# A first group cut into four tasks, other step orders at the layer change and in layer 1, and no restoring identity products: two chained GNN layers on one core

## The chip, the cores and the metric

The kernel runs on one core of a Trainium2 chip. The metric is the device time of one execution in microseconds (us), as the median of several executions. Lower is better.

## The reference

`x` is 128 graphs of 128 nodes with 512 features, `adj` 128 dense 128x128 adjacency matrices, all fp32. Layer 0 is a mean aggregation, layer 1 an attention-weighted diffusion with three hops. Both are followed by a residual and a layernorm:

```python
# layer 0
agg = einsum('bij,bjf->bif', adj, x) / max(sum(adj, -1), 1e-6)
x   = layernorm(x + relu(concat([x, agg], 2) @ W.T))          # W: 512 x 1024
# layer 1
Xw  = x @ Wv + bv                                             # used only through aw
e   = leaky_relu(sj[:, None, :] + si[:, :, None] + ab, 0.2)   # sj = Xw @ aw[:d], si = Xw @ aw[d:]
T   = adj * exp(e);  T = T / (sum(T, -1) + 1e-12)
H = 0; Xk = x
for k in range(3):
    H = H + Xk @ Wk[k] + bk[k]
    Xk = T @ Xk
x   = layernorm(x + relu(H))
```

## The kernel before

**Groups.** The 128 graphs are worked in 32 groups of 4 (`NG`, `G`): 32 periods of layer 0, then 32 of layer 1. The result of layer 0 goes through DRAM (`yd`) and is read back for layer 1, whose group 0 therefore needs only the early groups of layer 0.

**Products.** The large products with the weights are done by a scheme of seven products in place of eight block products, on two levels. The outer level gives tasks (`P12`, `P56`, `P74` and `T` in layer 0; `O1` to `O7` in layer 1), the inner level gives each task seven steps. A step is the matmuls of one inner product (`prod`, all recorded at line L149) and then the small work that this product releases. In layer 1 every `O` task runs `outer` (L605 to L641): after step 1 ScalarE copies bank X to Y (L617), after step 2 it copies Z to `s5` (L623), after step 3 VectorE adds W = X + s5 (L626), after step 5 it makes the sum Z directly (L650 or L663). Step 3 accumulates into X and must wait until the copy of step 1 has read it. Step 5 accumulates into X and must wait for the add of step 3, and step 7 for the direct sum of step 5. Steps 4 and 6 need the banks filled by the copy of step 1 and the add of step 3. `O5` starts its bank X from a copy of the folded bias (`beta`, L615). The tasks of kind `adding` also have GpSimd add into `s5` after step 3 (L660), and step 5's sum needs that. `C` combines the three hops (eight steps `c.1` to `c.8`, products with the transition matrix).

**Banks and lanes.** PSUM holds eight banks, four named bA and four named bB. Each four are a lane. A lane carries one task at a time, and two lanes alternate so that one task's small work lies beside the other's matmuls. All banks are first written by an identity product (L146).

**The order is written by hand.** `PA` (32 steps) is the order of a layer-0 period, `PT` that of the turn from layer 0 to layer 1, `PB` (57 steps) that of a layer-1 period, `PL` that of the last. In them a name with a small letter (`p74.6`, `t.1`, `o3.7`, `c.5`) is a step of the group before. In layer 1 the first group runs `PB` from `O5.1` on. Everything else (loads, transposes L254, left-side sums L242 to L277, layernorm L488 to L506, attention scores L712 to L721) is put beside the steps by `at` and `place`: the tables `START`, `PLACES_A`, `PLACES_B`, `PLACES_T`, `PLACES_M` and `PLACES_L` give each operation a position in half-steps. The engines run in the order so emitted: there is no scheduler that moves instructions.

```python
for t, (lane, name, g, k) in enumerate(steps):
    ...
    next(gens[name, g], None)                        # the step's matmuls and small work
    run([(f, *args) for f, args in beside.pop(2 * t, ())])
    run(late)                                        # evictions that wait for this step
    run([(f, *args) for f, args in beside.pop(2 * t + 1, ())])
```

**The start.** Group 0 of layer 0 has no aggregation task beside it. A task `F` (function `first`, 14 steps in bA) makes two columns of seven products, each product for the upper half `xu` and the lower half `xl` of the group's graphs. Its first step needs both. The group's first two transposes give `xu`, the next two `xl`; GpSimd makes the inner sums (`x_inner`, L242 to L245), VectorE the inner differences of the weights (`w_inner`, L931 to L934) and two of the outer ones (`w_outer`, L939). Bank set bB takes `fold_constants` meanwhile: biases and attention vectors are folded in seven small pieces (`fold`), and at the end two identity products (L184) write the two banks that the folding had used. `FL` then multiplies by the adjacency.

Of the kernel before, what the change touches and what calls it, by code (L numbers as in the profile page):

```python
# [8 lines left out]
FP = mybir.dt.float32  # L9
# [7 lines left out]
def kernel(  # L17
# [14 lines left out]
    nc = tc.nc  # L32
    P = 128
# [8 lines left out]
    R = 32  # L42
# [67 lines left out]
    wvt_sb = [p2.tile([P, 2, F], FP, name=f"wvt{i}", tag="y") for i in range(2)]  # L110
# [3 lines left out]
    bk_sb = p1.tile([K, F], FP, name="bk_sb", tag="TT")  # L114
# [5 lines left out]
    load_w0([nc.scalar], 1)  # L120
    load_w0([nc.scalar], 3)
    load_adj(0)
    for i in range(2):
        nc.sync.dma_start(wvt_sb[i], wvt[i * FH : (i + 1) * FH, :].rearrange("(c p) f -> p c f", p=P))
# [32 lines left out]
    def fold_constants():  # L157
        ones_row = ones[:].to_broadcast([P, P])
        pb, pc, pw = bB[0], bB[3], bB[0]
# [17 lines left out]
        w2row = p1.tile([2, NC, Q, R], FP, name="w2row", tag="TT")  # L177
# [5 lines left out]
        for t in (pw, pc):  # L183
            nc.tensor.matmul(t, ident, ident[:, None, :].to_broadcast([P, Q, P]), start=True, stop=True)  # L184
# [72 lines left out]
    def x_inner(n, p):  # L257
        need(("x_turn", n, p, 1))
        t = (xu, xl)[p][n]
        left_sums([S_, S_, S_, S_], [t[:, :, i] for i in range(7)])  # L260
# [71 lines left out]
    def p12(lane, g):  # L332
        r, c11 = rs[g], c11s[g] = blocks(p2, "r"), blocks(p2, "c11")

        def evict(b, t):
            L_.copy(part(r, b), t[:, :FH])
            V.tensor_add(part(c11, b), t[:, FH:], part(r, b))
        yield from pair(lane, g, 1, 2, evict)
# [10 lines left out]
    def p74(lane, g):  # L349
        r, c22, c21 = rs[g], blocks(p2, "c22"), blocks(p2, "c21")  # L350
        c22s[g], c21s[g] = c22, c21

        def evict(b, t):
            need(("P56", g, {BY: 4, BWW: 6, BZ: 7, BX: 7}[b]))
            L_.copy(part(c22, b), t[:, :FH])
            V.tensor_add(part(c21, b), t[:, FH:], part(r, b))
            V.tensor_add(part(c21, b), t[:, :FH], part(c21, b))
        yield from pair(lane, g, 7, 4, evict)
# [68 lines left out]
    def first(lane, g):  # L427
        c11, c21 = blocks(p2, "c11"), blocks(p2, "c21")
        c11s[g], c21s[g] = c11, c21

        def column(o, bank_of, evict):
            X, Y, W, Z = [bA[i] for i in bank_of]

            def prod(dst, k, start=False):
                for h in range(2):
                    for i in range(2):
                        mm(dst[:, h * FH : (h + 1) * FH], (xu, xl)[h][g][:, i, LEFT[k]], wf[:, SLOT[2 * i + o], RIGHT[k]],
                           start and i == h == 0)
            s5 = halves()
            prod(X, 1, True)  # L440
            L_.copy(Y, X)
            yield
            prod(Z, 5, True)
            L_.copy(s5, Z)
            yield
            prod(X, 6)
            V.tensor_add(W, X, s5)
            yield
            prod(Y, 2)
            yield  # L450
            prod(X, 7)
            evict(BY, Y)
            V.tensor_add(Z, X, s5)
            yield
            prod(W, 3)
            yield
            prod(X, 4)
            evict(BWW, W)
            evict(BZ, Z)
            late.append((evict, BX, X))  # L460
            yield

        def evict0(b, t):
            L_.copy(part(c11, b), t[:, :FH])
            V.tensor_copy(part(c21, b), t[:, FH:])
        yield from column(0, (0, 1, 2, 3), evict0)

        def evict1(b, t):
            i, h = b
            L_.copy(bB[i][:, h * FH : (h + 1) * FH], t[:, :FH])  # L470
            V.tensor_copy(bB[2 + i][:, h * FH : (h + 1) * FH], t[:, FH:])
        yield from column(1, (1, 2, 0, 3), evict1)
        lane[:] = [bA[2], bA[3], bA[1], bA[0]]

    def first_last(lane, g):
        new_mv(g)
        for p, t in ((1, c21s[g]), (0, c11s[g])):
            for i in range(2):
                b = 2 * p + i
                mm(bB[b], aTs[g][:, b], t[:, i, :, :FH])  # L480
                late.append((residual, g, b, bB[b]))
            yield
        lane[:] = [bB[2], bB[0], bB[1], bB[3]]
# [326 lines left out]
    TASKS = {"F": first, "FL": first_last, "P12": p12, "P56": p56, "P74": p74, "T": last, "O1": o1, "O2": o2, "O5": o5,  # L810
             "O6": o6, "O7": o7, "O4": o4, "O3": o3, "C": combine}
    lanes = [list(bA), list(bB)]
    steps = []

    def step(lane, name, g, k):
        steps.append((lane, name, g, k))

    PA = "p74.5 P12.1 P12.2 p74.6 P12.3 p74.7 P12.4 t.1 P12.5 P12.6 t.2 P12.7 P56.1 t.3 P56.2 t.4 t.5 P56.3 t.6 t.7 t.8 t.9 t.10 t.11 P74.1 P74.2 P56.4 P56.5 P56.6 P74.3 P56.7 P74.4".split()
    PT = "p74.5 O1.1 O1.2 p74.6 O1.3 O1.4 p74.7 t.1 t.2 O1.5 O1.6 O1.7 O2.1 t.3 O2.2 t.4 t.5 O2.3 t.6 t.7 t.8 t.9 t.10 t.11 O2.4 O2.5 O2.6".split()
    PB = ("o3.7 O1.1 O1.2 O2.1 O1.3 O2.2 O1.4 O1.5 O1.6 O1.7 O2.3 O2.4 O5.1 O5.2 O2.5 O5.3 O5.4 O2.6 O5.5 "  # L820
          "O2.7 O6.1 O5.6 O6.2 O5.7 O7.1 O6.3 O7.2 O6.4 O6.5 O7.3 O6.6 O6.7 O7.4 O4.1 O7.5 O4.2 O7.6 O4.3 "
          "O7.7 O4.4 O4.5 O4.6 c.1 O4.7 O3.1 c.2 O3.2 O3.3 O3.4 c.3 c.4 c.5 c.6 c.7 c.8 O3.5 O3.6").split()
# [3 lines left out]
    for k in range(14):  # L826
        step(0, "F", 0, k + 1)
# [18 lines left out]
    for g in range(NG):  # L846
        base[NG + g] = base[NG] + len(PB) * g
        for s in PB[PB.index("O5.1") if g == 0 else 0 :] if g < NG - 1 else PL:
# [16 lines left out]
    def place(n, pos, f, *a):  # L865
        at(2 * base[n] + pos, f, *a)

    PLACES_A = {
# [9 lines left out]
        ("y_store", 0, 1): 280, ("ln_var", 0, 2): 229, ("sum_r", 0, 1): 77, ("load_adj", 0): 129, ("ln_apply", 0, 0): 245,  # L878
        ("ln_apply", 0, 3): 257, ("ln_var", 0, 1): 229, ("load_y", 0, 0): 163, ("x_s2", 1): 71, ("ln_var", 0, 3): 233,
        ("t_load", 0): 125, ("x_turn", 1, 0, 0): 14, ("t_turn", 0): 189, ("sum_r", 0, 0): 85, ("x_turn", 1, 0, 1): 33,  # L880
        ("y_store", 0, 0): 258, ("load_y", 0, 1): 183, ("ln_apply", 0, 2): 270, ("ln_var", 0, 0): 231, ("t_back", 0): 158,
        ("t_exp", 0): 140, ("x_s4", 0): 43, ("ln_mean", 0): 224, ("sum_c", 0, 1): 106, ("ln_scales", 0): 233,
        ("sum_c", 0, 0): 114, ("t_sums", 0): 150, ("x_s3", 1): 84, ("x_s1", 1): 69, ("load_left", 2, 0): 66,
        ("x_turn", 1, 1, 0): 2, ("t_scores", 0): 116, ("t_norm", 0): 151, ("x_inner", 1, 0): 38, ("x_inner", 1, 1): 25,
        ("load_left", 2, 1): 38, ("x_turn", 1, 1, 1): 12, ("ln_apply", 0, 1): 256,
# [20 lines left out]
    for n in range(2 * NG):  # L906
        for (name, dn, *a), pos in (PLACES_A if n < NG else PLACES_B).items():
# [6 lines left out]
            place(n, pos, OPS[name], m - NG if name in OWN else m, *a)  # L914
# [10 lines left out]
    def fold(i):  # L925
        next(folding, None)
# [9 lines left out]
    def w_outer(i):  # L936
        need(("w_inner", 1), *{1: [], 2: [("w_outer", 1)], 3: [("F", 0, 14)], 4: [("w_outer", 2)]}[i])
# [4 lines left out]
        ("w_inner", 1): 9, ("x_s2", 1): 30, ("fold", 2): 3, ("a_turn", 0): 16, ("w_outer", 2): 16, ("fold", 4): 11,  # L942
        ("degree", 0): 10, ("a_norm", 0): 10, ("load_left", 1, 1): 9, ("x_s1", 1): 21, ("fold", 5): 16, ("fold", 3): 8,
        ("w_outer", 1): 11, ("fold", 7): 10, ("fold", 6): 17, ("x_s3", 1): 22, ("w_outer", 4): 19, ("load_y", 0, 0): 17,
        ("load_y", 0, 1): 9, ("x_turn", 1, 0, 0): 14, ("a_load", 0): 15, ("x_turn", 1, 0, 1): 14, ("x_inner", 1, 0): 16,
        ("x_turn", 1, 1, 1): 18, ("load_left", 1, 0): 12, ("x_turn", 1, 1, 0): 10, ("fold", 1): 4, ("x_inner", 1, 1): 19,
        ("w_outer", 3): 33, ("load_left", 2, 1): 19, ("load_adj", 1): 26, ("load_left", 2, 0): 23, ("load_wk",): 58,
    }
    OPS.update({f.__name__: f for f in (w_inner, w_outer, fold, load_wk)})
    for (name, *a), t in START.items():  # L950
        at(t, OPS[name], *a)
    PLACES_T = {
        ("wg_load", 1, 0): -488, ("wg_load", 1, 2): -406, ("wg_load", 1, 1): -453, ("wg_load", 2, 0): -346,
        ("wg_load", 2, 2): -274, ("wg_load", 2, 3): -259, ("wg_load", 6, 0): -27, ("wg_load", 5, 0): -215,
        ("wg_load", 5, 1): -183, ("wg_load", 5, 2): -156, ("wg_load", 5, 3): -107, ("wg_load", 6, 1): -20,
        ("wg_load", 1, 3): -382, ("wg_load", 6, 2): -11, ("wg_load", 6, 3): 15, ("wg_load", 4, 1): 45, ("wg_load", 7, 0): 13,
        ("wg_load", 4, 3): 58, ("wg_load", 7, 1): 19, ("wg_load", 7, 2): 28, ("wg_load", 7, 3): 42, ("wg_load", 4, 0): 36,
        ("wg_load", 4, 2): 64, ("wg_load", 3, 0): 65, ("wg_load", 3, 1): 67, ("wg_load", 2, 1): -311, ("wg_load", 3, 2): 80,
        ("wg_load", 3, 3): 87,
# [11 lines left out]
    for p in range(2):  # L971
        run([(x_turn, 0, p, 0), (x_turn, 0, p, 1)])
    run([(x_inner, 0, 0), (x_inner, 0, 1), (w_inner, 0)])
# [43 lines left out]
```

## Time and profile before

| what | us |
|---|---|
| median of 3 runs | 2112.71 (2112.41 to 2116.83) |
| the profiled execution | 2111.64 |
| its span | 2109.8 |
| TensorE busy | 2083.5 |
| VectorE busy | 1464.6 |
| GpSimd busy | 1539.4 |
| ScalarE busy | 1145.5 |
| layer-0 period (start of P12.1 to the next) | 24.74 |
| layer-1 period (start of O1.1 to the next) | 39.53 |
| window 11.25 to 61 (start): TensorE busy | 45.62 of 49.75 |
| window 816 to 861 (layer change): TensorE busy | 40.14 of 45 |

The span runs from the first to the last record of the profiled execution; 1.84 us of that execution's time lie around it. In the timeline a row joins neighbouring instructions of one kind, and its columns are start, busy time, engine, line, tile, shape, count, and in brackets the idle time before it with what ended it. Matmuls overlap at their ends, so the time that a row takes from the engine is read from its start to the start of the next row. An undisturbed step of 385 columns is two records and takes 0.647 us so, one of 256 columns twice 0.216, one of 512 columns twice 0.430.

### The profile page before, as it was taken

What the parts mean: (1) busy time and instruction counts of PE and PEld (TensorE: products, weight loads), DVE (VectorE), ACT (ScalarE), POOL (GpSimd) and SP (SyncE); (2) the same over time, 40 slices, a digit from 0 to 9 for tenths busy, and PEclk for the clock granted to TensorE, in tenths of its full rate; (3) what the DMA queues carried; (4) which work ended last, traced back from release to release, by engine and by line L of the source; (5) the groups of instructions that cost most, each with busy time, mean ns of one, the idle gap of its engine ahead of it and who ended that gap; (6) DMA issues with size and microseconds to landing.
All of it is one profiled execution on the core that took longest, in us unless ns stands there. A gap on an engine that the chain in (4) does not pass through costs nothing.

```text
span 2109.8 us, 25967 instructions
## 1 busy us (share of the span) xinstructions
PE 2083.5 (99%) x7104; PEld 1328.1 (63%) x7104; DVE 1464.6 (69%) x3235; ACT 1145.5 (54%) x2879; POOL 1539.4 (73%) x1432
## 2 busy tenths in 40 slices
PE   8999999999999999999999999999999999999997
PEld 5887888888778886555555555555555555555553
DVE  4778777777777776666666666666666666666665
ACT  2665666666656665355455455455455455455454
POOL 5877888887767776767767767767767767767763
PEclk9999999999999999999999999999999999999999
DMA  7766666566566768334434434434434434434423
GB/s 177 183 186 190 189 184 173 159 190 192 160 173 182 191 164 239 76 91 121 109 91 119 112 91 121 109 91 120 111 91 120 111 91 120 111 91 121 110 71 115
DMA packets 429486, 287.13 MB, mean 136 GB/s; under 512 B 153497, under 2 KB 352281, under 8 KB 429340
## 3 DMA queue, kind: packets, MB, share of 16 engines
q1 hardware_dynamic: 428092, 283.62, 50.7%
q10 hardware_dynamic: 1120, 1.84, 0.4%
q8 instruction: 56, 0.92, 0.2%
q14 instruction: 90, 0.74, 0.1%
q0 software_dynamic: 128, 0.01, 0.0%
HBM read 191.60 MB, written 93.79 MB: 135 GB/s over the span
## 4 chain that ended last, share of the span: by engine, by line
PE 95%; DVE 2%; POOL 1%; DMA 1%; ACT 1%; issue 0%; ACTq 0%; SPq 0%; POOLq 0%; DVEq 0%
PE bB L149 50%; PE bA L149 45%; DVE y L371 1%; DVE r L663 1%; DMA xb<-in_x_dram 0%; DMA big<-wd 0%; DMA big<-in_w0t_dram 0%; PE bB L174 0%; POOL s L660 0%; ACT junk L493 0%; POOL r L696 0%; ACT T L762 0%; POOL xs L265 0%; POOL xs L269 0%; POOL xu L277 0%
## 5 line engine op out<-in xcount | busy, mean ns | idle before, releaser
L149 PE MATMUL bA<-big,xu 128*128 128x256 f32 (+1 forms) x1834 | 578.6, 435 | 3.3 <-DVE r L663 1.0
L149 PEld LDWEIGHTS bA<-big,xu 128*128 128x128 f32 x1834 | 345.6, 190 | 177.6 <-issue 25.7
L149 PE MATMUL bB<-big,xl 128*128 128x256 f32 (+1 forms) x1330 | 399.1, 416 | 0.2 <-ACT bB L617 0.2
L149 PE MATMUL bA<-big,xs 128*128 128x256 f32 (+1 forms) x1316 | 387.9, 418 | 0.2
L149 PEld LDWEIGHTS bB<-big,xl 128*128 128x128 f32 x1330 | 252.0, 190 | 99.3 <-issue 15.5
L149 PEld LDWEIGHTS bA<-big,xs 128*128 128x128 f32 x1316 | 245.1, 190 | 92.1 <-DVE bA L626 14.3
L149 PE MATMUL bB<-big,xu 128*128 128x256 f32 (+1 forms) x868 | 286.1, 440 | 2.6 <-DVE bB L388 2.5
L149 PE MATMUL bB<-c,TT 128*128 128x512 f32 x512 | 246.3, 594 | 0.0
L660 POOL TENSOR_TENSOR s<-s,r 128x385 f32<-128x385 f32 x128 | 127.6, 997 | 151.2 <-DVE bA L626 105.3
L493 ACT ACTIVATE junk<-y,mv 128x512 bf16<-128x512 f32 x252 | 181.6, 721 | 78.6 <-POOL mv L488 74.5
L149 PEld LDWEIGHTS bB<-big,xu 128*128 128x128 f32 x868 | 159.0, 189 | 91.7 <-DVE r L650 19.3
L506 ACT ACTIVATE y<-y,mv,rstd 128x512 f32<-128x512 f32 x252 | 201.4, 811 | 1.3 <-POOL mv L501 1.3
L626 DVE TENSOR_TENSOR bA<-bA,s 128x385 f32<-128x385 f32 x128 | 72.5, 567 | 165.6 <-ACT s L623 117.8
L149 PE MATMUL bA<-big,xl 128*128 128x385 f32 (+1 forms) x490 | 181.3, 476 | 4.2 <-DVE xl L254 4.1
L371 DVE SCALAR_TENSOR_TENSOR y<-bB,y 128x512 f32<-128x512 f32 x256 | 170.4, 682 | 19.8 <-PE bB L149 13.5
L149 PE MATMUL bB<-big,xs 128*128 128x385 f32 x448 | 173.5, 492 | 0.9 <-POOL xl L242 0.9
L149 PEld LDWEIGHTS bB<-c,TT 128*128 128x128 f32 x512 | 97.2, 190 | 89.4 <-issue 48.6
L797 ACT COPY bB<-r 128x512 f32<-128x512 f32 x64 | 37.7, 589 | 193.4 <-DVE big L796 188.2
L277 POOL TENSOR_TENSOR xu<-xu,xs 128x896 f32<-128x896 f32 x63 | 131.3, 2085 | 10.3 <-PE bA L149 10.3
L149 PEld LDWEIGHTS bA<-big,xl 128*128 128x128 f32 x490 | 93.3, 191 | 71.0 <-DVE c L663 7.9
L273 POOL TENSOR_TENSOR xl<-xu,xl 128x896 f32<-128x896 f32 x63 | 133.3, 2116 | 1.1
L269 POOL TENSOR_TENSOR xs<-xs,xu 128x896 f32<-128x896 f32 x63 | 131.7, 2090 | 2.4
(172 smaller groups left out, 3540.3 us busy)
## 6 DMA issues: line engine op xcount, KB each, us to landing
xb<-in_x_dram SPq DMA_DIRECT2D x256, 128.0 KB, 3.5
y<-in_x_dram SPq DMA_DIRECT2D x64, 512.0 KB, 4.5
yd<-y SPq DMA_DIRECT2D x64, 512.0 KB, 2.8
xb<-yd SPq DMA_DIRECT2D x256, 128.0 KB, 3.9
y<-yd SPq DMA_DIRECT2D x64, 512.0 KB, 4.4
out_dram<-y SPq DMA_DIRECT2D x62, 512.0 KB, 2.8
ag<-in_adj_dram SPq DMA_DIRECT2D x64, 256.0 KB, 4.0
sb<-sd SPq DMA_DIRECT2D x252, 64.0 KB, 3.1
```

The lines of the kernel that those rows point to most:

```text
L149: nc.tensor.matmul(dst, lhsT, rhs, start=start, stop=True, skip_group_check=True)
L269: S_.tensor_sub(xs[n][:, 1], xs[n][:, 0], xu[n][:, 0])
L273: S_.tensor_sub(xl[n][:, 0], xu[n][:, 0], xl[n][:, 0])
L277: S_.tensor_sub(xu[n][:, 1], xu[n][:, 1], xs[n][:, 1])
L371: V.scalar_tensor_tensor(y, t, 0.0, y, ALU.max, ALU.add, accum_out=mvs[n][:, b, 0:1])
L493: L_.activation(junk, ys[n, b // 2][:, b % 2], AF.Square, bias=mvs[n][:, b, 0:1], accum_out=mvs[n][:, b, 1:2])
L506: L_.activation(y, y, AF.Identity, bias=mvs[n][:, b, 0:1], scale=rstds[n][:, b : b + 1])
L626: V.tensor_add(W, X, s5)
L660: S_.tensor_add(s5, s5, part(src, BZ, BW))
L663: V.tensor_add(part(dst, BZ, BW), X, s5)
L797: L_.copy(at_[b], row(b, 254, 766, 1))
```

## The change

**Start.** `F` becomes four tasks of seven steps: A and B for the first column (upper half, lower half), C and D for the second. Each works in half banks: A and B in bA, C and D in bB, A and C in the first 256 columns. The order is the new list `PF` (28 steps); A needs only `xu`. The sums `x_inner(0, .)` go from GpSimd to VectorE. The loads of the last two quarters of the weights are issued by ScalarE and SyncE in turn, no longer by ScalarE alone. The load of `wvt` and the seven pieces of folding move behind the first group, into slots of group 1's period that were empty, in banks bA[2] and bA[3]; the two identity products go. The two lanes swap their bank sets.

**Layer change.** `PT` has a new order. The first layer-1 group has an order of its own, `PG`, in place of a part of `PB`. A table `PLACES_S` gives the operations around the change positions of their own, and `PLACES_T` (weight loads) is re-timed.

**Layer 1.** `PB` has a new order and `PLACES_B` new positions. The last group keeps `PL`, layer 0's periods keep `PA` and `PLACES_A`, `outer` and the other tasks are the same.

The core of the diff:

```diff
-    load_w0([nc.scalar], 1)
-    load_w0([nc.scalar], 3)
+    load_w0([nc.scalar, nc.sync], 1)
+    load_w0([nc.scalar, nc.sync], 3)
...
     def fold_constants():
         ones_row = ones[:].to_broadcast([P, P])
-        pb, pc, pw = bB[0], bB[3], bB[0]
+        need(("FL", 0, 2))
+        pb, pc, pw = bA[2], bA[3], bA[2]
...
-        for t in (pw, pc):
-            nc.tensor.matmul(t, ident, ident[:, None, :].to_broadcast([P, Q, P]), start=True, stop=True)
         yield
...
-        left_sums([S_, S_, S_, S_], [t[:, :, i] for i in range(7)])
+        left_sums([S_ if n else V] * 4, [t[:, :, i] for i in range(7)])
...
-    def first(lane, g):
...
+    def first(g, o, h):
+        X, Y, W, Z = [t[:, h * FH : (h + 1) * FH] for t in (bA, bB)[o]]
...
+        def prod(dst, k, start=False):
+            for i in range(2):
+                mm(dst, (xu, xl)[h][g][:, i, LEFT[k]], wf[:, SLOT[2 * i + o], RIGHT[k]], start and i == h == 0)
...
+    PF = "A.1 A.2 A.3 A.4 A.5 A.6 B.1 B.2 B.3 C.1 B.4 A.7 C.2 B.5 C.3 B.6 B.7 C.4 C.5 C.6 D.1 D.2 D.3 D.4 D.5 D.6 C.7 D.7".split()
...
-    PT = "p74.5 O1.1 O1.2 p74.6 O1.3 O1.4 p74.7 t.1 t.2 O1.5 O1.6 O1.7 O2.1 t.3 O2.2 t.4 t.5 O2.3 t.6 t.7 t.8 t.9 t.10 t.11 O2.4 O2.5 O2.6".split()
-    PB = ("o3.7 O1.1 O1.2 O2.1 O1.3 O2.2 O1.4 O1.5 O1.6 O1.7 O2.3 O2.4 O5.1 O5.2 O2.5 O5.3 O5.4 O2.6 O5.5 "
-          "O2.7 O6.1 O5.6 O6.2 O5.7 O7.1 O6.3 O7.2 O6.4 O6.5 O7.3 O6.6 O6.7 O7.4 O4.1 O7.5 O4.2 O7.6 O4.3 "
-          "O7.7 O4.4 O4.5 O4.6 c.1 O4.7 O3.1 c.2 O3.2 O3.3 O3.4 c.3 c.4 c.5 c.6 c.7 c.8 O3.5 O3.6").split()
+    PT = "p74.5 p74.6 O1.1 O1.2 O1.3 p74.7 O1.4 t.1 O1.5 O1.6 t.2 O1.7 O2.1 t.3 O2.2 t.4 t.5 O2.3 t.6 t.7 t.8 t.9 t.10 t.11 O2.4 O2.5 O2.6".split()
+    PG = ("O5.1 O5.2 O5.3 O5.4 O2.5 O2.6 O6.1 O6.2 O5.5 O5.6 O5.7 O7.1 O6.3 O6.4 O7.2 "
+          "O6.5 O2.7 O7.3 O6.6 O7.4 O6.7 O4.1 O4.2 O7.5 O4.3 O7.6 O7.7 O4.4 c.1 O4.5 "
+          "O4.6 c.2 c.3 c.4 O4.7 O3.1 O3.2 O3.3 O3.4 c.5 c.6 c.7 c.8 O3.5 O3.6").split()
+    PB = ("O1.1 o3.7 O1.2 O1.3 O2.1 O2.2 O1.4 O1.5 O1.6 O1.7 O2.3 O2.4 O5.1 O5.2 O5.3 O2.5 O2.6 O5.4 O5.5 "
+          "O2.7 O6.1 O5.6 O6.2 O5.7 O7.1 O6.3 O7.2 O6.4 O6.5 O7.3 O6.6 O6.7 O7.4 O4.1 O4.2 O7.5 O4.3 O7.6 "
+          "O4.4 O7.7 O4.5 c.1 c.2 O4.6 O4.7 O3.1 O3.2 c.3 c.4 O3.3 c.5 O3.4 c.6 c.7 c.8 O3.5 O3.6").split()
...
+    lanes = [[bB[1], bB[3], bB[0], bB[2]], list(bA)]
...
+    PLACES_S = {
+        ("ln_apply", -2, 3): 4, ("ln_var", -2, 0): -9, ("sum_c22", -2): -40, ("ln_scales", -2): -1, ("ln_mean", -2): -15,
+        ("ln_var", -2, 2): -4, ("load_y", -2, 1): -27, ("ln_apply", -2, 2): 10, ("ln_var", -2, 1): -4,
...
+        ("ln_mean", -1): 48, ("x_turn", 0, 0, 0): -28, ("ln_var", -1, 2): 55, ("load_y", -1, 1): 38, ("load_y", -1, 0): 40,
...
     PLACES_B = {
...
-        ("t_load", 0): 125, ("x_turn", 1, 0, 0): 14, ("t_turn", 0): 189, ("sum_r", 0, 0): 85, ("x_turn", 1, 0, 1): 33,
-        ("y_store", 0, 0): 258, ("load_y", 0, 1): 183, ("ln_apply", 0, 2): 270, ("ln_var", 0, 0): 231, ("t_back", 0): 158,
+        ("t_load", 0): 118, ("ln_var", 0, 0): 230, ("ln_apply", 0, 3): 255, ("x_turn", 1, 0, 0): 12, ("ln_scales", 0): 244,
+        ("y_store", 0, 0): 262, ("ln_apply", 0, 2): 274, ("load_left", 2, 1): 59,
...
     START = {
-        ("w_inner", 1): 9, ("x_s2", 1): 30, ("fold", 2): 3, ("a_turn", 0): 16, ("w_outer", 2): 16, ("fold", 4): 11,
+        ("fold", 2): 81, ("x_inner", 0, 1): 13, ("load_y", 0, 0): 7, ("fold", 5): 86, ("fold", 4): 85, ("degree", 0): 23,
+        ("fold", 3): 81, ("x_s2", 1): 54, ("a_norm", 0): 25, ("x_turn", 1, 0, 0): 30, ("fold", 6): 91, ("x_s1", 1): 48,
+        ("w_outer", 1): 22, ("w_outer", 2): 34, ("w_outer", 4): 37, ("load_wvt",): 32, ("fold", 7): 102,
...
-    for p in range(2):
-        run([(x_turn, 0, p, 0), (x_turn, 0, p, 1)])
-    run([(x_inner, 0, 0), (x_inner, 0, 1), (w_inner, 0)])
+    run([(x_turn, 0, 0, 0), (x_turn, 0, 0, 1), (x_inner, 0, 0), (w_inner, 0)])
```

## Prediction

> **What bounds the kernel now.** I read the page's busy times first, then the waits of TensorE, then its timeline in the three places that the change touches.
>
> ```profile
> PE 2083.5 (99%) x7104; PEld 1328.1 (63%) x7104; DVE 1464.6 (69%) x3235; ACT 1145.5 (54%) x2879; POOL 1539.4 (73%) x1432
> ```
>
> TensorE is the bound in every stage, so the change is worth what it takes out of TensorE's idle time and out of its products, and nothing else. Busy time hides short stalls, because a row's end overlaps the next; I take rows from start to start against the undisturbed step (0.647 us for 385 columns, 0.216 for a 256-column record, 0.861 for a 512-column product). Summed over all rows that way, 59.5 us of the 2109.8 us span are not products at full speed.
>
> The waits, and the **start**:
>
> ```profile
> PE bA L149 <- DVE xl L254: 4.1, 1, 4.1
> PE bB L149 <- DVE bB L388: 2.5, 1, 2.5
> PE bA L149 <- DVE r L663: 1.0, 1, 1.0
> PE bB L149 <- POOL xl L242: 0.9, 1, 0.9
> ...
> 16.41 2.08 PE L149 MATMUL bA<-big,xl 128*128 128x256 f32 x4 [4.13 <-DVE xl L254]
> ...
> 39.31 1.98 PE L184 MATMUL bB<-ident 128*128 128x512 f32 x4
> ...
> 15.93 1.28 ACT L441 ACT_TABLE_LOAD   x1 [15.93 <-DMA big<-in_w0t_dram]
> ```
>
> F.1 has done its upper half at 12.1 us and waits 4.13 us for the transposes of `xl`. The next 8 records (16.41 to 19.81) take 3.4 us in place of 1.73. The identity products take 1.8 us (39.31 to 41.13).
>
> The **layer change** (816 to 861 us) idles longest at T.2, O5.1 and O3.7, the second to fourth wait. What is behind O5.1 is not GpSimd's sum, as the wait has it, but ScalarE's queue:
>
> ```profile
> 831.80 0.72 ACT L493 ACTIVATE junk<-y,mv 128x512 bf16<-128x512 f32 x1 [5.98 <-POOL mv L488]
> 832.43 0.19 ACT L493 ACTIVATION_READ_ACCUMULATOR junk<-y,mv 128x1 f32 x1
> 832.52 0.47 ACT L615 COPY bB<-beta 128x385 f32<-128x385 f32 x1
> ```
>
> The beta copy, which O5.1 accumulates onto, stands behind a layernorm row that had waited for GpSimd; TensorE starts at 833.10.
>
> **Layer 1** is 1189 us and shows no wait at all in that list, yet a period takes 39.53 us where 49 steps of 0.647 and 8 of 0.861 make 38.57: 0.96 is lost in pieces.
>
> ```profile
> 1015.57 2.44 PE L149 MATMUL bA<-big,xu 128*128 128x385 f32 x6
> 1017.85 1.46 PE L149 MATMUL bB<-big,xu 128*128 128x385 f32 x4
> ...
> 1021.09 3.02 PE L149 MATMUL bB<-big,xu 128*128 128x385 f32 x8
> 1023.94 1.46 PE L149 MATMUL bA<-big,xu 128*128 128x385 f32 x4
> 1025.32 1.53 PE L149 MATMUL bB<-big,xs 128*128 128x385 f32 x4
> 1026.68 0.81 PE L149 MATMUL bA<-big,xu 128*128 128x385 f32 x2
> ...
> 1016.49 0.56 DVE L663 TENSOR_TENSOR r<-bA,s 128x385 f32<-128x385 f32 x1
> ```
>
> Six records from 1015.57 should reach 1017.51, not 1017.85: 0.34 lost (O3.6 to o3.7; one step lies between O3.5 and o3.7, and the sum L663 of 0.56 plus its hand-overs is longer than that step). Eight from 1021.09 lose 0.26 (O1.5 to O1.7, the same), O5.1 loses 0.09 and 0.06. The mean over 30 periods is 0.97: o3.7 0.341, O1.7 0.272, O5.1 0.153, O6.5 0.134, c.8 0.072. Each stall ends with one slow record (0.07 to 0.105, counted in).
>
> [...]
>
> **Start, step by step.** Task A needs only `xu`, so its six steps (each four 0.216-us records, 0.86) run on from 11.25 to 16.4. ScalarE issues 10 weight loads, not 14: its issues end at 8.38 + 10/14 of 7.52, at 13.75 if they are even, sooner if the first go faster; then 1.28 of table load, and the copy of A.1 can follow by 11.8 to 15. I take the early end, with A.3 at 13.0. B.1 waits for `xl`: landing at 15.56, two transposes and their waits on VectorE to 17.8, some 1.4 us idle, less than the 2.48 that left the clock alone at T.2. B.7 waits about 1.0 behind `w_inner(1)` (2.7) and `w_outer(1)` (1.98) on VectorE; P12.3 0.2 behind GpSimd's `w_outer`, then `x_inner`. P12.7 of group 1 then ends near 48.5 instead of 59.5 - 5.9 (53.6); but the folding (8 small groups, 4.5 to 4.9 us of TensorE with their switches, before inside the first 59.5) now stands after it. Equal work is reached at 53.4 in place of 59.48: **6.1 us less**, of which 1.8 are the identity products, 4.1 + 1.7 the old wait and its slow clock, less 2.6 of new waits, and the rest the small switches between `F` and the folding. The `wvt` load moves on SP to a slot where loads for group 1 follow, which have over 10 us in hand. Bounds: 4 (copy of A.1 late by 2 us) to 8 (B.7 not waiting).
>
> **Layer change.** T.2's add waits at L388 behind L356/L357, whose ScalarE copies stand behind four `ln_apply` of 0.81. In the new order these lie elsewhere and O1.5 and O1.6 stand before t.2: 0.35 remains of 2.75. O5.1 (1.14) goes, because the group's `ln_var` rows now follow it. O3.7 (1.27, behind GpSimd's 1.81 + 2.07 + 1.81 ahead of L660) shrinks to 0 to 0.35: GpSimd still has 0.98 + 1.81 + 1.81 + 2.07 in a row there, but it begins at O4.3, nine steps (5.8 us) ahead of O3.3, and O1.1 stands as one more step before O3.7. The order puts new one-step covers in: O5.3, O5.7, O4.7, O3.3, O3.5 at 0.23 to 0.34 each, about 1.35 together; the small old ones (0.09 to 0.45: O1.7, O5.5, O7.3, O6.7, O4.7, O3.x) went from 2.45 to that. Loss 7.6 before, 2.1 + 0.2 after: **5.3 us less**, bounds 3 and 6.5. What could come late is `y` of group 31: y_store, load_y (4.5 to land) and T.8's residual; T.8 comes 3 us earlier, and I find 1 to 2.5 us left. The weight loads moved on SP by up to 16 half-steps (some 5 us) keep more than that.
>
> **Layer 1, 30 periods.** O1.1 now stands between O3.6 and o3.7: two steps of cover (1.29) against 0.9 of hand-over and sum, so 0.341 goes, in 29 periods. c.8's 0.072 goes (two or three more steps between c.5 and c.8). `ln_apply(2)` moves four half-steps later, out of the way of O6.2's copy, and O6.5's 0.134 goes. O5.3 has only O5.2 between it and O5.1, whose copy (0.47 and hand-overs 0.52 and 0.15, 1.13 from the record's start) needs more than one step gives: a new 0.23, as the same pattern cost at O3.3 in the layer change (854.36). O1.7 and O5.1 stay. So 0.97 becomes 0.655: 0.316 x 29 = **9.2 us less**.
> The unknown in it is O1.5. Its add W waits for the `s5` copy of O1.2, which ScalarE's queue holds behind three `ln_var` (0.85 each), the copy of O1.1 and `t_scores`. Worked through, W is ready 5.11 us after O3.6's start and O1.5's turn comes at 5.18. With 0.07 in hand it may stall 0 to 0.35 a period. Behind it on VectorE wait a transpose and later sums only, with a step to spare; on TensorE everything. I charge 0.08 in the mean, 2.5 us, with 0 and 10 as ends. The transition row (`t_load`) lands 0.4 us before `t_exp` needs it, which itself has over 1 us before TensorE asks; the `xb` loads have 8 us. The moves on GpSimd (`sum_r`, `x_s`) stay in order with the O3 and O6 sums behind, and it is busy 865 of 1189 us here.
>
> **Sum.** 6.1 + 5.3 + 9.2 - 2.5 = 18.1. The profiled execution (2111.64) would be 2093.5; the median lies 1.07 above it, so 2094.6. I say 2094.5. The layer-0 periods, the last group and the tail are the same.
>
> **Rivals.**
> 1. *The stall of o3.7 only moves on* (chance 0.2). Then O1.5 waits 0.3 for ScalarE's queue and layer 1 gains nothing: 2112.7 - 11.4 = 2101.3. For it: the 0.07 in hand; against: the queue's durations vary by less than 0.1.
> 2. *The start gives half* (0.12). ScalarE's issues end late, A.3 waits as F.1 did, or the clock falls in B.1's wait and costs 1.7: gain 2 to 4, total 2097 to 2099.
> 3. *Slower* (0.05). ScalarE's queue at O1.2 is late by a whole further `ln_var`. Without it layer 1 still has to give back 11.4 (start and change) and 4.2 more, over 30 periods 0.52 beyond today's 0.97, which is 0.52 above rival 1's 0.3 at O1.5, about 0.83 in all. That is one `ln_var` (0.85) standing before the copy that I have put behind it: 2117. Against it: at most three rows were emitted ahead of it.
> 4. *The change doesn't do what it says* (0.02): a `need` or a tile's reuse orders A behind `xl` after all, and the orders cost as before: 2111 to 2113. The instruction streams do show A's steps ahead of B's on TensorE.
>
> **How the numbers follow.** The main case has 0.61 and spans 2089 to 2098 by its own bounds; with rivals 1 and 2 the range is 2088 to 2103. A measurement of this kernel tells 0.2% (4.2 us) from no change. Faster by more than that: main case and rivals 1 and 2, 0.93; within it: rival 4 and the mildest of 3, 0.03; slower: 0.04.
>
> **What would show it.** Right: no wait on `xl` above 2 us, TensorE clock at full after 12 us, no L184 row, P56.7 of group 1 some 6 us earlier; T.2's row without 2.48; O1.1 to the next O1.1 in 39.2 us or a little more, o3.7 following O1.1 without a stall and one of 0.23 at O5.3. Wrong: a period of 39.5 or longer (rival 1, with the stall before O1.5), or a start row at half clock.

## The result and the profile after

| | before | after |
|---|---|---|
| median, us | 2113.29 (2112.41 to 2116.83, 4 runs) | 2094.57 (2093.66 to 2094.93, 4 runs) |
| ratio | | 0.9908, 95% interval 0.989 to 0.9925 |
| the profiled execution / its span | 2111.64 / 2109.8 | 2093.66 / 2091.9 |
| layer-1 period, mean of 27 (O1.2 of group 3 to group 30) | 39.55 | 39.22 |

The change is faster by 0.92%; 2094.5 was forecast. The busy times of the engines hardly differ:

```profile
PE 2074.7 (99%) x7100; PEld 1330.3 (64%) x7100; DVE 1465.5 (70%) x3247; ACT 1153.7 (55%) x2883; POOL 1532.2 (73%) x1424
```

TensorE is busy 8.8 us less and its span is 17.9 us shorter. The rest was idle time, as the waits of TensorE show (releaser, then total, times, longest):

```profile
PE bB L151 <- DVE r L670: 0.5, 1, 0.5
PE bB L151 <- ACT bA L452: 0.4, 1, 0.4
PE bB L151 <- DVE c L670: 0.3, 1, 0.3
PE bA L151 <- DVE bA L471: 0.3, 1, 0.3
```

Of the four waits shown of before (4.1, 2.5, 1.0, 0.9) three are gone, and the third, that of O3.7 at the layer change, has shrunk to the 0.5 in the first row. The other rows are D.7, O4.7 and B.7. The longer ones that are not shown (2.7 for the identity, 2.2 in the tail) lie in both kernels.

TensorE's timeline of the start:

```profile
2.66 6.52 PE L148 MATMUL bA<-ident 128*128 128x512 f32 x8 [2.66 <-POOL ident masks.py:199]
...
12.45 5.34 PE L151 MATMUL bA<-big,xu 128*128 128x256 f32 x24
17.63 2.89 PE L151 MATMUL bA<-big,xl 128*128 128x256 f32 x12
...
26.84 1.13 PE L151 MATMUL bA<-big,xl 128*128 128x256 f32 x4 [0.28 <-DVE bA L471]
...
37.05 1.13 PE L151 MATMUL bB<-big,xl 128*128 128x256 f32 x4 [0.45 <-ACT bA L452]
```

Task A runs without a gap and B follows at once (17.63), with the granted clock at 1.00 from 8.37 on; two short waits stand at B.7 and D.7. Before, the eight identity records in bA took 5.33 us and F.1 began at 11.25; here they took 6.52 and A.1 begins at 12.45, and that is not the change's doing (below).

The same stretch of a layer-1 period as was shown of before:

```profile
1006.13 1.46 PE L151 MATMUL bB<-big,xu 128*128 128x385 f32 x4
1007.43 0.81 PE L151 MATMUL bA<-big,xu 128*128 128x385 f32 x2
1008.07 0.81 PE L151 MATMUL bB<-big,xu 128*128 128x385 f32 x2
1008.72 1.46 PE L151 MATMUL bA<-big,xu 128*128 128x385 f32 x4
1010.02 1.46 PE L151 MATMUL bB<-big,xu 128*128 128x385 f32 x4
1011.31 3.07 PE L151 MATMUL bA<-big,xu 128*128 128x385 f32 x8
1014.22 1.46 PE L151 MATMUL bB<-big,xu 128*128 128x385 f32 x4
1015.60 2.35 PE L151 MATMUL bA<-big,xs 128*128 128x385 f32 x6
1017.78 1.46 PE L151 MATMUL bB<-big,xu 128*128 128x385 f32 x4
```

O3.5, O3.6, O1.1 and o3.7 (1006.13 to 1008.72) keep to 0.647 a step. O1.4 to O1.7 take 2.91 in place of 2.59 (0.05 in O1.5 and the old 0.27 at O1.7), then 0.085 ahead of O5.1, then O5.1 to O5.3 take 2.18 in place of 1.94: 0.07 in O5.1 and the new 0.17 at O5.3.

By stages, from equal steps in the two profiled executions (how much earlier the changed kernel reaches a step):

| stage, to the start of | gain here | forecast |
|---|---|---|
| start, P12.1 of group 2 | 5.36 | 6.1 |
| layer 0, P74.5 of group 31 | -0.69 | 0 |
| layer change, O1.2 of layer-1 group 1 | 4.19 | 5.3 |
| layer 1 and the end, last record | 9.10 | 6.7 |
| sum | 17.96 | 18.1 |

So the total was met in part by luck: errors of both signs cancel. The two profiled executions were also alike in their last task, where others of the 14 lose up to 1.4 us more (last section).

### The profile page after: what moved, and what is told of

Same layout as the page of the kernel before. It is cut to its first block, busy times and chain, and to the rows that moved or that the text cites. A ratio compares the mean times of both kernels' runs of the same rounds, so it can differ in the third digit from the quotient of the medians.

```text
span 2091.9 us, 25884 instructions
## 1 busy us (share of the span) xinstructions
PE 2074.7 (99%) x7100; PEld 1330.3 (64%) x7100; DVE 1465.5 (70%) x3247; ACT 1153.7 (55%) x2883; POOL 1532.2 (73%) x1424
## 4 chain that ended last, share of the span: by engine, by line
PE 96%; DMA 1%; POOL 1%; DVE 1%; ACT 0%; issue 0%; ACTq 0%; DVEq 0%; POOLq 0%
PE bA L151 50%; PE bB L151 45%; DMA big<-in_w0t_dram 1%; DMA yd<-y 0%; DMA xb<-in_x_dram 0%; DMA y<-in_x_dram 0%; PE bA L177 0%; POOL s L667 0%; POOL c L711 0%; POOL r L703 0%; ACT junk L500 0%; DVE y L376 0%; POOL xs L266 0%; POOL xs L270 0%; POOL xu L278 0%
## 5 line engine op out<-in xcount | busy, mean ns | idle before, releaser
L151 PE MATMUL bB<-big,xu 128*128 128x385 f32 (+1 forms) x1806 | 562.1, 434 | 0.7 <-DVE r L670 0.5
L151 PEld LDWEIGHTS bB<-big,xu 128*128 128x128 f32 x1806 | 341.8, 190 | 167.7 <-issue 44.8
L151 PE MATMUL bA<-big,xl 128*128 128x256 f32 (+1 forms) x1358 | 405.8, 416 | 0.4 <-DVE bA L471 0.3
L151 PE MATMUL bB<-big,xs 128*128 128x256 f32 (+1 forms) x1316 | 384.1, 416 | 0.0
L151 PEld LDWEIGHTS bB<-big,xs 128*128 128x128 f32 x1316 | 249.1, 190 | 84.8 <-ACT bB L624 6.2
L151 PE MATMUL bA<-big,xu 128*128 128x256 f32 (+1 forms) x896 | 294.3, 440 | 0.4 <-DVE bA L633 0.2
L151 PE MATMUL bA<-c,TT 128*128 128x512 f32 x512 | 241.3, 593 | 0.0
L151 PEld LDWEIGHTS bA<-big,xu 128*128 128x128 f32 x896 | 162.0, 189 | 95.4 <-DVE r L657 19.3
L151 PE MATMUL bA<-big,xs 128*128 128x385 f32 x448 | 173.7, 499 | 0.0
L151 PE MATMUL bB<-big,xl 128*128 128x385 f32 (+1 forms) x462 | 172.0, 480 | 0.8 <-ACT bA L452 0.4
L624 ACT COPY bB<-bB 128x385 f32<-128x385 f32 x128 | 60.1, 470 | 143.8 <-PE bB L151 143.8
```

What stands on the lines that cost most here:

```text
L151: nc.tensor.matmul(dst, lhsT, rhs, start=start, stop=True, skip_group_check=True)
```

## The experiments

Each median is compared with runs of the kernel before on the same chip, whose medians were 2110.36 to 2111.94. A stall is the time that a step of TensorE starts late, read from start to start; a 0.104 or less behind a "+" is the slow record that follows a stall, and a stall given as one number has it counted in. The cover of a step is the number of steps that stand between it and the product whose small work it needs.

**start_alone.** The changed file with `PT`, `PB`, `PLACES_B` and `PLACES_T` of before, `PG` cut from that `PB`, `PLACES_S` empty.

```diff
-    PLACES_S = {
...
+    PLACES_S = {}
+    PG = PB[PB.index("O5.1") :]
```

> The changed start (four tasks, folding moved, no identity products) with the orders and tables of before for the layer change and layer 1. Theory (the parts add up): P12.1 of group 2 starts 5.4 us earlier than before, as in the changed kernel, layer change and layer-1 period (39.53) as before, so about 2113.3 - 5.4 = 2107.9. The slow drift of layer 0 in the changed kernel (its period is 0.012 us longer, 0.3 us over 28 periods) comes from the swap of the bank sets and is seen here too: gain 5.0 at P12.1 of group 31. Rival A (the start is hidden behind the loads, and the gain is lost within layer 0): 2112 to 2113.5. Rival B (the re-timing around the layer change makes the drift): no drift here.

Measured: 2106.16 against 2111.88, ratio 0.9976 (0.9967 to 0.9984). P12.1 of group 2 starts 5.65 earlier than in the profile of before and P12.1 of group 31 still 5.61: no drift, so not the swap of the banks. It is not the re-timing either: ident_back has the tables of the changed kernel and keeps 4.25 and 4.21. In the one profiled execution of the changed kernel every period was some 0.05% longer (39.224 against 39.207 in ident_back). That accounts for 0.34 of the -0.69; the rest is a new stall at T.4 of group 30 (0.21 + 0.10) that ident_back has too and start_alone has not: a cost of the re-timing. From there the gain stays at 5.5 up to the last group: the start's gain does not rest on the new orders. In the last task 1.4 of it goes again. The first row is the changed kernel's, the second that of start_alone:

```profile
2075.41 3.46 PE L151 MATMUL bA<-c,TT 128*128 128x512 f32 x6
2087.91 4.84 PE L151 MATMUL bA<-c,TT 128*128 128x512 f32 x6
```

The same six records of `C` take 1.38 longer. In the changed kernel's profile the granted clock was 0.50 from 2073.44 to 2076.85, 1.44 into its row; that it came up later in start_alone is an estimate from the length of the row. The new order of the layer change was not run alone: its 4.19 is read from the equal steps above.

**layer1_alone.** The kernel before with the new `PB` and `PLACES_B` from the second layer-1 group on.

```diff
-        for (name, dn, *a), pos in (PLACES_A if n < NG else PLACES_B).items():
+        for (name, dn, *a), pos in (PLACES_A if n < NG else PLACES_G if n == NG else PLACES_B).items():
```

> The kernel before with only the new order PB and table PLACES_B from the second layer-1 group on. Theory: each of 29 periods gets 0.33 us shorter (39.20), 9.6 in all, about 2103.7, whatever the start and the layer change do. Rival (the gain of layer 1 rests on the changed start and change, say on loads that come earlier): the period stays above 39.35 and the time above 2108.

Measured: 2103.86 against 2111.88, ratio 0.9966 (0.9953 to 0.9979), period 39.21. The layer-1 order does its work without the other two parts. Its median falls by 8.0, not by 29 times 0.35. In its profiled execution O1.5 of group 2 waits 0.88, and the last task is as slow as in start_alone; how much of the difference these make in the median is not shown. The profile also shows the old start with other luck:

```profile
12.37 1.03 PE L149 MATMUL bA<-big,xu 128*128 128x256 f32 x4
16.64 1.13 PE L149 MATMUL bA<-big,xl 128*128 128x256 f32 x4 [3.24 <-DVE xl L254]
```

F.1 starts at 12.37, idles 3.24 and goes on with four records in 0.97 (16.64 to 17.61); P12.1 of group 2 comes 1.34 earlier than in the profile of before, where the idle time was 4.13, the granted clock 0.50 from 16.20 to 19.61, and the four records took 1.87.

**o11_first.** The kernel before with O1.1 ahead of o3.7, and `t_scores` half a step later, so that it still follows o3.7.

```diff
+    PN = ["O1.1", "o3.7"] + PB[2:]
...
-        ("x_turn", 1, 1, 0): 2, ("t_scores", 0): 116, ("t_norm", 0): 151, ("x_inner", 1, 0): 38, ("x_inner", 1, 1): 25,
+        ("x_turn", 1, 1, 0): 2, ("t_scores", 0): 117, ("t_norm", 0): 151, ("x_inner", 1, 0): 38, ("x_inner", 1, 1): 25,
```

> The kernel before with one swap: in the layer-1 groups 1 to 30, O1.1 stands before o3.7 (and t_scores goes half a step later, so that it still follows O3's last step); all other steps and positions stay. Theory (o3.7's stall is one step of cover too few): o3.7's 0.34 goes and nothing replaces it but up to 0.05 at O1.5: period 39.19 to 39.24, 8.5 to 9.9 us less, 2103.4 to 2104.8. Rival (the stall only moves on to O1.5, whose copy stands behind layernorm rows on ScalarE): a stall of 0.2 to 0.35 at O1.5, period 39.4 to 39.53, 2109.5 to 2113.3.

Measured: 2127.42 against 2111.88, slower, ratio 1.0075 (1.0058 to 1.0092). o3.7's 0.34 is gone and O1.5 waits 0.78 + 0.10 in every period (40.10): worse than either expectation. The waits name VectorE's add (L626), but that had idled itself; ScalarE's timeline tells what it waited for:

```profile
979.20 0.46 ACT L617 COPY bB<-bB 128x385 f32<-128x385 f32 x1 [3.15 <-PE bB L149]
979.58 0.72 ACT L493 ACTIVATE junk<-y,mv 128x512 bf16<-128x512 f32 x1
...
980.43 0.72 ACT L493 ACTIVATE junk<-y,mv 128x512 bf16<-128x512 f32 x1
...
981.27 0.72 ACT L493 ACTIVATE junk<-y,mv 128x512 bf16<-128x512 f32 x1
...
982.56 0.46 ACT L623 COPY s<-bB 128x385 f32<-128x385 f32 x1
```

ScalarE idles 3.15 us for O1.1's copy, which now comes first, and only then makes three layernorm rows and the scores; O1.2's copy to `s5`, which O1.5's add needs, starts at 982.56, 3.36 after O1.1's. In the changed kernel one of the three rows stands ahead of O1.1's copy:

```profile
1007.39 0.72 ACT L500 ACTIVATE junk<-y,mv 128x512 bf16<-128x512 f32 x1 [2.84 <-POOL mv L495]
...
1008.27 0.47 ACT L624 COPY bA<-bA 128x385 f32<-128x385 f32 x1
1008.65 0.73 ACT L500 ACTIVATE junk<-y,mv 128x512 bf16<-128x512 f32 x1
...
1009.50 0.72 ACT L500 ACTIVATE junk<-y,mv 128x512 bf16<-128x512 f32 x1
...
1010.79 0.46 ACT L630 COPY s<-bA 128x385 f32<-128x385 f32 x1
```

There it is 2.52 after it, 0.84 less: the row fills time in which ScalarE would wait for O1.1. Whether it is the cause was tested next.

**o11_lnvar.** o11_first and one move more.

```diff
-        ("y_store", 0, 1): 280, ("ln_var", 0, 2): 229, ("sum_r", 0, 1): 77, ("load_adj", 0): 129, ("ln_apply", 0, 0): 245,
+        ("y_store", 0, 1): 280, ("ln_var", 0, 2): 225, ("sum_r", 0, 1): 77, ("load_adj", 0): 129, ("ln_apply", 0, 0): 245,
```

> The swap of o11_first (O1.1 before o3.7) and one move more: the layernorm row ln_var(2) two steps earlier (position 229 to 225), so that on ScalarE it stands ahead of O1.1's copy and not behind it. Theory (o11_first lost because three ln_var rows and t_scores stood between O1.1's copy and the s5 copy that O1.5's add needs; one of them out of it is 0.85): the stall of 0.79 + 0.10 at O1.5 falls to 0 to 0.06, o3.7 keeps no stall, period about 39.2, total 9 to 10 below before, 2102 to 2103. Rival A (t_scores, which waits for o3.7's last sum, decides alone): the stall at O1.5 stays above 0.5, total above 2117. Rival B (the order O1.3 ahead of O2.1 is needed too): a stall of 0.2 to 0.4, total about that of before.

Measured: 2103.40 against 2111.92, ratio 0.9959 (0.9944 to 0.9974). O1.5 loses 0.04, o3.7 nothing, the period is 39.25. One row's place on ScalarE turns +15.5 into -8.5 us. These two edits give layer 1's gain nearly whole; the new `PB`'s others take away O6.5's and c.8's 0.2 and add O5.3's 0.17.

**ident_back.** The changed kernel with the two identity products put back behind the folding.

```diff
         L_.copy(stage[:, :, 3 * F : 3 * F + 2], pc[:, : 2 * NC].rearrange("p (c t) -> p c t", c=NC))
+        for t in (pw, pc):
+            nc.tensor.matmul(t, ident, ident[:, None, :].to_broadcast([P, Q, P]), start=True, stop=True)
```

> The changed kernel with the two restoring identity products put back behind the last piece of folding. Theory (TensorE has no gap there): P12.1 of group 2 starts 1.7 to 1.9 us later counted from A.1's start (52.1 us in the changed kernel), the total is 1.8 higher. Rival (the products lie in a wait, for the copy of w2row or a switch): 0 to 0.5. If the clock comes up at another moment in the first identity products, A.1 starts at another time than 12.45; that shift is read separately.

Measured: from A.1's start to P12.1 of group 2 53.80 in place of 52.09, 1.71 more: four records of 0.43, nothing hidden. Its single time, 2094.91, is only 0.3 above the median after. A.1 began at 11.85 there in place of 12.45, and the last task differs by up to 1.45 between executions (last section), so one time doesn't tell the products' price; the trace does.

**o53_cover.** The changed kernel with O2.5 between O5.2 and O5.3.

```diff
-    ... "O1.1 o3.7 O1.2 O1.3 O2.1 O2.2 O1.4 O1.5 O1.6 O1.7 O2.3 O2.4 O5.1 O5.2 O5.3 O2.5 O2.6 O5.4 O5.5 "
+    ... "O1.1 o3.7 O1.2 O1.3 O2.1 O2.2 O1.4 O1.5 O1.6 O1.7 O2.3 O2.4 O5.1 O5.2 O2.5 O5.3 O2.6 O5.4 O5.5 "
```

> The changed kernel with O2.5 put between O5.2 and O5.3 (the order of before at this place) in the layer-1 periods. Theory (O5.3 stalls because only O5.2 lies between it and O5.1's copy): its 0.072 + 0.104 go, period 39.03 in place of 39.20, 5 less, about 2089.5. Rival (O2.5, now one step earlier, waits for GpSimd's sum in its turn, or O5.1's late beta copy holds up both): period above 39.15, 2093 to 2095.

Measured: 2092.00, ratio 0.9905 (0.9888 to 0.9921) to before, period 39.16. O5.3's 0.17 is gone, but O5.5, which needs the add of O5.3 and now has two steps of cover and not three, waits 0.02 + 0.104. So of 0.17 only 0.05 is left as gain, near the rival.

**pool_first.** The changed kernel with `x_s2(1)` and `x_s3(1)` behind `sum_c` at the layer change.

```diff
-        ("x_s2", 1): 99, ("x_s4", 0): 80,
+        ("x_s2", 1): 147, ("x_s4", 0): 80,
...
-        ("x_s3", 1): 127, ("x_inner", 1, 0): 64,
+        ("x_s3", 1): 149, ("x_inner", 1, 0): 64,
```

> The changed kernel with two GpSimd operations of layer-1 group 1 put later at the layer change: x_s2(1) from position 99 to 147 and x_s3(1) from 127 to 149, both behind the attention sums sum_c of group 0. Theory (GpSimd's queue, busy without a gap from 835 to 853.7, makes the stalls O4.7 0.59, O3.7 0.80 and O1.5 0.46 there): from O5.1 of group 0 to O1.2 of group 1 26.97 falls to 25.6, and O1.2 of group 2 comes 1.8 earlier by the same count. Rival (VectorE or ScalarE holds these steps): less than 0.3.

GpSimd at the layer change, first in the changed kernel, where its queue has no gap, then here:

```profile
840.56 2.09 POOL L270 TENSOR_TENSOR xs<-xs,xu 128x896 f32<-128x896 f32 x1
842.60 1.00 POOL L667 TENSOR_TENSOR s<-s,c 128x385 f32<-128x385 f32 x1
843.56 3.59 POOL L703 TENSOR_TENSOR r<-r,s 128x770 f32<-128x770 f32 x2
847.10 2.09 POOL L274 TENSOR_TENSOR xl<-xu,xl 128x896 f32<-128x896 f32 x1
849.15 0.99 POOL L667 TENSOR_TENSOR s<-s,r 128x385 f32<-128x385 f32 x1
```

```profile
847.12 1.00 POOL L667 TENSOR_TENSOR s<-s,r 128x385 f32<-128x385 f32 x1 [1.91 <-DVE bB L633]
```

Measured: one run, 2091.26. O3's sum no longer stands behind `x_s3`; O3.7's 0.80 is gone, O4.7 falls from 0.59 to 0.34, O1.5 from 0.46 to 0.26. From O5.1 to O1.2 of group 1 it is 26.14 in place of 26.97: 0.83, not 1.4, as O5.3 waited 0.47 there in place of 0.26 for ScalarE's copy. To O1.2 of group 2 it is 1.05, not 1.8. GpSimd's queue is shown as the cause of most of these stalls, not of all; the two operations were moved together, so what each is worth is not shown.

**two_covers.** pool_first with two steps of cover in the pairs O1.5 to O1.7, O5.1 to O5.3 and O5.3 to O5.5, and O5's bias copy emitted ahead of O1.7's last eviction (an operation `beta_in` at position 20).

```diff
+    PB = ("O1.1 o3.7 O1.2 O1.3 O2.1 O2.2 O1.4 O1.5 O1.6 O2.3 O1.7 O2.4 O2.5 O5.1 O5.2 O2.6 O5.3 O5.4 O2.7 "
+          "O5.5 O6.1 O5.6 O6.2 O5.7 O7.1 O6.3 O7.2 ...
```

> The changed kernel with pool_first's two moves and, in the layer-1 periods, the order O1.5 O1.6 O2.3 O1.7 O2.4 O2.5 O5.1 O5.2 O2.6 O5.3 O5.4 O2.7 O5.5, which puts two steps between the pairs O1.5-O1.7, O5.1-O5.3, O5.3-O5.5; and the beta copy of O5.1's bank is emitted ahead of O1.7's last eviction on ScalarE. Theory (each of these stalls is one step of cover too few, or a place in ScalarE's queue): of the 0.64 a period loses 0.0 to 0.1 is left, period 38.6 to 38.7, 15 to 17 less in layer 1 and 1.8 at the layer change: 2076 to 2078. Rival (as in o11_first, the stalls move on to the next late step, to O2.5 behind GpSimd's sum or O5.3): period above 39.0, 2088 or more.

Measured: 2099.48, ratio 0.994 (0.9925 to 0.9955), period 39.46: slower than the changed kernel. The stalls aimed at are gone (which move took which is not shown), and O5.3 waits 0.78 + 0.10:

```profile
1016.49 1.28 ACT L758 ACTIVATE T<-T,si 128x128 f32<-128x128 f32 x4 [0.74 <-DMA T<-scd]
1017.79 0.63 ACT L760 ACTIVATE T<-T 128x512 f32<-128x512 f32 x1
1018.33 0.47 ACT L624 COPY bA<-bA 128x385 f32<-128x385 f32 x1
```

`t_exp` kept its position, but O5.1 moved one step behind it: its copy (L624) now stands after T's load and 1.9 us of rows.

**covers_exp, covers_exp2, covers_all, covers_all2.** Four steps from there, each moving what the trace before it showed ahead of the late operation: `t_exp` to 141; `t_exp` to 140 and `ln_apply(3)` to 263; besides that `t_sums` to 153 and `t_norm` to 154; besides that `x_inner(1, 0)` to 42.

The entries of `PLACES_B` at the end of the four, put together:

```diff
-        ("t_norm", 0): 151, ("t_exp", 0): 139, ("t_sums", 0): 150, ("ln_apply", 0, 3): 255, ("x_inner", 1, 0): 36,
+        ("t_norm", 0): 154, ("t_exp", 0): 140, ("t_sums", 0): 153, ("ln_apply", 0, 3): 263, ("x_inner", 1, 0): 42,
```

> two_covers with t_exp put one step later in the layer-1 periods (position 139 to 141), so that its rows on ScalarE (1.28 + 0.63, and the wait for the transition row's load) stand behind O5.1's copy and not ahead of it. Theory (in two_covers these rows held the copy of O5.1 from 1015.7 to 1018.33, the stall of 0.78 + 0.10 at O5.3, and nothing else was left in the period): the stall goes, 0.04 to 0.1 lost in a period, 38.6 to 38.7, 2076 to 2078. Rival (the later t_exp makes T late for c.1, or the two ln_apply rows behind it hold O5.4's eviction and so O5.5 or O6.3): a stall of 0.2 to 0.8 elsewhere, 2082 to 2100.

covers_exp measured: 2124.72, ratio 1.0061 (1.0047 to 1.0075): O5.7 waits 1.58 + 0.10. Two `ln_apply` rows (1.5) came ahead of `t_exp`; T's row sum waits for it on VectorE, and the sum for O5.7 stands behind that.

> two_covers with t_exp half a step later (139 to 140, so directly behind O5.1's copy and ahead of the two ln_apply rows that delayed it in covers_exp) and one of these, ln_apply(3), four steps later (255 to 263, behind O5.4's eviction). Theory (in covers_exp the two ln_apply rows, 1.5 us, made T late, so that VectorE's row sum of T, which waits for it, held the sum that O5.7 needs, 1.58 + 0.10): both the stall at O5.3 and that at O5.7 go, at most 0.2 a period is left, period 38.6 to 38.8, 2076 to 2083. Rival (ScalarE has no place for t_exp in this stretch without a step of TensorE waiting): a stall of 0.4 or more at O5.7, O6.3 or O6.5, 2086 or more.

covers_exp2 measured: 2082.09, ratio 0.9855 (0.9839 to 0.9872), period 38.89, 0.18 + 0.10 left at O5.7.

> covers_exp2 with the row sum and the scaling of T later in the layer-1 periods (t_sums position 150 to 153, t_norm 151 to 154), so that VectorE makes the sum that O5.7 needs ahead of the reciprocal and not behind it, and ScalarE copies O6.1's bank ahead of T's scaling. Theory (what is left in covers_exp2, 0.18 + 0.10 at O5.7, is VectorE's queue): it goes, and only 0.04 at O1.5 and perhaps up to 0.1 at O6.5, whose copy now stands behind the scaling, are left: period 38.6 to 38.7, 2074 to 2077. T's turn in VectorE has 3.5 us in hand. Rival (the scaling now holds O6.2's copy, and the stall moves on to O6.5): 0.25 to 0.4 there, 2081 to 2085.

covers_all measured: 2128.26, ratio 1.0078 (1.0061 to 1.0094): O6.3 waits 0.78 + 0.10 and O7.2 0.82 + 0.10. T's product with the adjacency had come behind four sums of 0.72 on GpSimd (1021.75 to 1024.73), which neither expectation had.

> covers_all with x_inner(1, 0) six half-steps later (36 to 42), so that on GpSimd the product of adjacency and T stands ahead of these four sums of 0.72 and not behind them. Theory (in covers_all they held T's product from about 1021.9 to 1024.7, and with it the row sum, the scaling and on ScalarE the copies that O6.3 and O7.2 need): both stalls there go, 0.04 to 0.3 a period is left, 2074 to 2082. Rival (the sums now hold x_s4 and GpSimd's sum for O6.5, or O3 of the group): a stall of 0.3 or more at O6.5 or later, 2083 to 2095.

covers_all2 measured: 2074.59 against 2110.36, ratio 0.9828 (0.981 to 0.9845), period 38.61 of 38.57 possible; only O1.5's 0.04 is left. It beats both kernels.

## Why the prediction was right, and where its steps were not

**What bounds the kernel** held: TensorE in every stage. In every experiment with several executions the median moved with the gaps between TensorE's starts, to within some 2 us; the two ends of the kernel differ by execution about as much (1.6 at the start of A.1 or F.1, 1.45 in the last task). Of the cases named, the main one came.

**Start, 6.1 forecast, 5.36 here, 5.65 in start_alone.** The old wait with its slow clock (from 11.25 to 19.81, less twelve records of 0.216) was worth 5.96, and the products 1.71, as said. Five terms were off. *B.1's wait of 1.4* didn't come: the step counted two transposes of `xl`, but B.1 uses only what the first one writes (done at 16.35, while A ran to 17.63). *D.7* (0.61 + 0.10) was missed: it writes the other half of the bank from which ScalarE had still to evict C.7 (36.64 to 37.00), and starts at 37.05; that this sharing is the reason is read from the order of the two, no run took it apart. *B.7* cost 0.55, not about 1.0. *The small switches* between `F` and the folding, the 1.1 that the step's sum leaves for "the rest", came to 0.4: in the new place the folding pays for its switches too. Counted from the start of A.1 and of F.1, P12.1 of group 2 then comes after 52.09 in place of 58.65, 6.56 less.

The fifth term is *A.1 at 11.25*, which was taken from the one profile of before. It began at 12.45 here, and between 11.04 and 12.65 in the 14 profiled executions, whichever kernel: the eight identity records in bA took 5.12 where it was 11.04 and 6.72 where it was 12.65. Its 12.45 takes 1.20 off again, so that the 5.36 is near the forecast in part by luck. It is also counted from an execution of before in which the clock fell to 0.50 in the wait (16.20); against the two executions of the old start in which it did not, P12.1 of group 2 comes only 4.0 and 4.1 earlier. The rival "the start gives half" did not come.

**Layer change, 5.3 forecast, 4.19 here.** O5.1's stall went as said, and T.2's went whole, where the step had left 0.35. *O3.7 at 0 to 0.35* measured 0.80, and *O4.7, one of five at 0.23 to 0.34,* measured 0.59. The step let GpSimd's row of work begin at O4.3, with nothing ahead of it. O4.3 started at 839.89, yet `x_s1` and `x_s2` (4.2 us) kept GpSimd busy until 842.60. pool_first, which takes `x_s2` and `x_s3` out of the row, shows that the queue is the cause. O2.7 (0.30), O1.3 (0.24) and O5.5 (0.26) were not counted, and O1.5 of group 1 (0.46, behind `sum_c` and the scores) falls under layer 1.

**Layer 1, 6.7 forecast, 9.1 here.** The period fell by 0.33: o3.7, O6.5 and c.8 gone as listed, O1.7 and O5.1 unchanged, O5.3 and O1.5 new. The terms that failed are the sizes of the last two, and both were too high. O5.3 was listed at 0.23 and is 0.17, which makes 1.6 in 29 periods: the step gave 0.15 to the hand-over from ScalarE's copy to the product that waits for it, and here O5.3 starts 0.05 after the end of that copy. O1.5 was charged with 2.5; it lost 0.05 (a slow record) in each of 29 periods and 0.46 in group 1, 1.9 in all. The 0.07 in hand was enough, so rival 1 did not come.

But the reason given for o3.7's gain was only half of it. The step named the two steps of cover; it counted ScalarE's rows ahead of O1.5, and did not say that one of them had to change sides for the gain to come. o11_first has the cover alone and is 15.5 us slower: rivals 1 and 3 as they were described, the stall moved to O1.5 and deeper than it had been. The price put on rival 3 (one `ln_var`, 0.85, from which the whole turns slower) is what o11_first and o11_lnvar differ by: 40.10 - 39.25.

**Layer 0, 0 forecast, -0.69 here**: half is that one execution, half T.4 of group 30, which start_alone, without the re-timing, does not have.

## What to carry to other kernels

When one step more of cover takes a stall away, work out what the move puts ahead of each late copy in the other engines' queues: the same swap cost 15.5 us or gained 8.5 with one 0.85 us row on the other side of a copy. An operation placed at a fixed position changes its place in the queue when the order around it changes, though nobody moved it: read each engine's order anew after each move, its waiting rows first. And split a small gain by stages at equal steps of two traces before believing the sum: here 0.7, 1.1 and 0.7 too little hid 2.4 too much.

## What the runs showed of the hardware

In the profile of before TensorE's granted clock comes up to 1.00 at 5.96, is 0.50 from 16.20 to 19.61 and from 2091.50 to 2094.92, and falls again at 2105.16. In that of the changed kernel it comes up at 8.37, is 0.50 from 2073.44 to 2076.85, and falls again at 2087.09. In these two profiles the stretches between the changes are 3.41, 10.24, 2065.06 and 2071.89 us: 1, 3, 605 and 607 times 3.4133.

Where the changes lie differs between the two. The first identity product starts at 2.65 or 2.66 in all 14 profiles, and the clock came up 3.30 us later in that of before and 5.71 later in that of the changed kernel. The weight loads of the identity products start 0.86 apart before that moment and 0.43 apart after it. The eight records in bA take 5.12 us (covers_all2) to 6.72 (two_covers); from these lengths and the two profiles the clock came up between about 5.5 and 8.8 in the 14, an estimate.

With the old start the idle time inside F.1 was 4.13 us in before, 4.23 in o11_first, 3.24 in layer1_alone and 3.40 in o11_lnvar. The four records after it took 1.87 and 1.86 us in the first two and 0.97 and 0.96 in the other two; the clock of before fell to 0.50 in that idle time. In layer1_alone and o11_lnvar P12.1 of group 2 came 1.25 to 1.34 earlier though F.1 had started 1.1 later. After the 2.48 us of idle time at T.2 in before the clock was still 1.00. What decides whether it falls is not shown.

`w_inner` (L931) took 1.16 us at 10.79 in before, beside GpSimd's sums, and 0.68 at 28.13 with GpSimd idle. In the changed kernel, where GpSimd is idle until 25.93, the same subtraction (L967) takes 0.69 at 11.38.

At the end the 3.41 us at half clock begin between the second and the third of the last group's waits in its attention (2.22, 0.54 and 0.35 in before, 2.23, 0.54 and 0.36 after). From O4.7 to the last step of `C` it takes 13.19 to 14.64 us in the 14 profiles, 13.19 in that of before and 13.22 in that of the changed kernel. So part of the spread of before (2109.95 to 2116.83 over all its runs) can come from the two ends; that was not tested by itself.
